# A top-1 expert layer fed by a scan: rows written to their expert places by scatters, read back in order, with routing and weight folding between the last scans

## The chip, the cores and the metric

The kernel runs on one core of a Trainium2 chip. The metric is device time in microseconds (us) of one execution. A core has five engines that run side by side, each working through its own instructions in order and waiting on semaphores for the others: PE (TensorE, matrix multiplies and transposes), DVE (VectorE, elementwise work, reductions and scans), ACT (ScalarE, activation functions and copies), POOL (GpSimd, elementwise work and the issue of indirect DMAs) and SP (SyncE, which here only issues DMAs). SBUF is the on-chip memory of 128 partitions, PSUM the banks into which PE writes, HBM (or DRAM) the memory outside.

## The reference, cut to what matters

The whole program is a chain of eight layers over 2048 tokens of 128 channels: an RG-LRU scan, a local-attention transformer of two blocks, a Mamba layer, a first mixture of experts (top-1 of 32), a chunked attention block, a second mixture of experts, an attention layer with decay and a ternary linear layer. A layer norm stands between layers. The change touches the joint between Mamba and the first experts:

```python
# Mamba, per sequence of 256 tokens: 256 inner channels, 16 states
delta = softplus(delta_raw * w_dt + b_dt)
h = exp(delta * A) * h + delta * B_t * xc        # scan over the tokens
y = sum_n h[n] * C_t[n];  y = y + xc * D_param
out = (y * silu(z)) @ W_out

# first experts: E = 32, capacity C = ceil(1.25 * 2048 / 32) = 80
logits = xt @ w_router
probs  = softmax(logits);  top1 = argmax(probs);  gate = probs[top1]
pos = cumsum(onehot(top1), axis=0)[token, top1] - 1
accepted = pos < C
slot = where(accepted, top1 * C + pos, E * C)
buf = zeros(E * C + 1, H).at[slot].set(xt)       # each token to its place
y = (silu(buf @ w_gate) * (buf @ w_up)) @ w_down # per expert, 80 places
out = xt + where(accepted, y[slot] * gate, 0)
```

The place of a token depends on all tokens before it, so the last tokens' places are known only after the last sequence has passed through Mamba.

## The kernel before

**Layout and stages.** Activations are kept by channel (128 partitions of channels, tokens along the free axis) in fp32. The tokens are 8 sequences of 256, or 16 tiles of 128. Stages follow each other in the program: `rglru`, `local_mamba`, `moe1`, `chunked`, `moe2`, `typed`. In the profiled execution RG-LRU takes 0 to 52 us, local attention with Mamba runs to about 912, the routing of the last tokens, the fetching of rows and the first experts run to about 983, the chunked block to about 1437, the second experts to 1650 and the last two layers to the end. The program text is turned into five instruction streams by a scheduler, which may hoist an instruction within its stream; on the chip every stream runs in order.

**Mamba.** `interleave` mixes the generators of the local blocks (`one_sequence`) with those of `mamba_sequence`, at most two of the latter at a time, by lags written out by hand. In a sequence, `d` (delta) is made by ACT (L747 to L750), finished by four POOL instructions (L752 to L756, the last gives `u`), and then eight steps follow, `m` = 0 to 7. A step needs two broadcast rows `bc` (B and C of two states, read by SP from the small DRAM tensor `xs` of the sequence; three buffers of `bc`), the decay `da` (ACT, L767), three DVE instructions on 128x1024 values (L769 multiply by B, L771 scan, L772 multiply by C) and PE's sum `y`. After the last step come L778 (DVE), L779 (POOL, times the gate `sz`), `wout` (PE), the sum `s` and a layer norm. Its end `x_mamba` is transposed to rows (L790), copied to SBUF and stored to the DRAM tensor `rows1` by `put_rows` (SP), and the router's logits `lg` are computed (L803 copies them out).

**Routing and fetching.** `route1(0, 14)` routes the first 14 tiles, whose logits are in `lg1[0]`, and `route1(14, 16)` the last two. Each finds the largest logit, a one-hot `sel`, the position within its expert by triangular and all-ones matmuls (`cum`), and the place `sc`. To turn places into a list "which token sits in place i" it builds comparison matrices (`ge`, `at`, `column`, `value`) and multiplies them on PE (`which`), giving `index` (L1045). `rows_of` then has POOL fetch the 2560 places as 20 gathers of 128 rows each from `rows1` by `index` (L1112; 12 buffers), and PE transposes each to channels (L1104), with one copy `bt` for four.

**First experts.** `moe1` goes through eight groups of four experts: `pg` and `pu` (gate and up matmuls), `sg` (silu on ACT, multiplied by `pu` on DVE), `py` (down), a copy `ys` and a store to `ybuf`. A group's weights are 768 KB in three DMAs of 256 KB on SP (`weights1`); three buffers hold them, so three groups are loaded ahead and the other five follow as buffers come free. The chunked block begins by gathering each token's result from `ybuf` (POOL, `got<-ybuf,get`), two tiles a sequence, with `combined` adding it to the residual.

**Folding.** The chunked block's attention weights are multiplied together beforehand by `fold` (128 matmul records on PE and eight copies on ACT for two layers, from four raw loads `w_attn` of 1 MB each, plus `less`, 16 records for each layer, and one DVE subtraction `la_res`, `sa_res` for each). In the program text it stands between the two calls of `route1`, behind all sequences; the scheduler moves the parts. `bias_rows` splits a bias into three bf16 parts.

**Loads beside the last sequence.** `among` runs one step of `loads` at each step of the last Mamba sequence: weights of group 0, three raw loads, groups 1 and 2, `w_ffn` (1 MB), and the constants `cst` and `w3`.

Of the kernel before, what the change touches and what calls it, by code (L numbers as in the profile page):

```python
# [20 lines left out]
P = 128  # L21
# [283 lines left out]
class _Kernel:  # L305
    def __init__(self, ctx, tc, ins, out):
# [14 lines left out]

        self.scope = ctx.enter_context(ExitStack())
# [32 lines left out]

        self.get1 = const.tile([P, NT], I32, name="get1")
        self.gate1 = const.tile([P, NT], F32, name="gate1")
        self.sum1 = const.tile([P, 32], BF, name="sum1")
        self.which1 = const.tile([P, 40], F32, name="which1")
        self.index1 = const.tile([P, 20], I32, name="index1")  # L360
# [5 lines left out]
        nc.sync.dma_start(self.w1, ins["w1"])  # L366

# [36 lines left out]

    def exp_ln(self, last=None):

        i = self.nc.scalar.preload_act_table_set("natural_log_exp_and_others")
        if last is not None:
            self.issue_after([i], last)
        self.tc.keep_in_program_order(i)  # L410

# [59 lines left out]
    def rglru(self):  # L471
        nc, tc = self.nc, self.tc
        self.y = self.xs.tile([P, T], F32, tag="x", name="x_rglru")
        with tc.tile_pool(reuse_waits="tile", name="l0", bufs=1) as w, tc.tile_pool(reuse_waits="tile", name="l0t", bufs=2) as wk:

            c1 = self.softplus(w, self.v("apar"), 1, "sp")
            nc.vector.tensor_scalar(self.c12[:, 0:1], c1, -8.0, None, ALU.mult)
            nc.vector.tensor_scalar(self.c12[:, 1:2], c1, -16.0, None, ALU.mult)
            tiles = [w.tile([P, 4, S], F32, name=f"rg{i}") for i in range(4)]
            for _ in self.rglru_group(0, tiles, wk):  # L480
                pass
# [215 lines left out]
    def mamba_sequence(self, b, x, y, na, das, work, scan):  # L697
# [54 lines left out]
        nc.gpsimd.tensor_sub(e, e, t)  # L752
        nc.gpsimd.tensor_add(d, d, e)
        nc.gpsimd.tensor_add(d, d, r)
        u = tile("u", 2)
        nc.gpsimd.tensor_mul(u, d, xc)  # L756
# [22 lines left out]
        nc.gpsimd.tensor_mul(yg, yg, sz)  # L779
# [8 lines left out]
        ps = self.psum("B", "rows")[:, 0:S]  # L788
        for t in range(2):
            nc.tensor.transpose(ps[:, t * P : (t + 1) * P], y[:, b * S + t * P : b * S + (t + 1) * P], self.ident)  # L790
        r = work.tile([P, S], F32, tag="h2", name="rows")
        nc.any.tensor_copy(r, ps)
        self.put_rows(b, r)
        self.logits(b, y, self.w1[:, 834:866], self.lg1[0][:, 2 * b : 2 * b + 2] if b < 7 else self.lg1[1])
        yield 1.0
# [13 lines left out]
    def local_mamba(self):  # L809
        nc, tc = self.nc, self.tc  # L810
        self.rows = self.dram.tile([T, P], F32, name="rows1")
        w = self.w0
        with (
# [4 lines left out]
            ExitStack() as tail,  # L818
# [50 lines left out]
            def then(value):  # L869
                b, z = value  # L870
                if b == 0:

                    self.x = self.xs.tile([P, T], F32, tag="x", name="x_mamba")
                steps = self.mamba_sequence(b, z, self.x, na, das, work, scan)
                return steps if b < 7 else among(steps, loads())

            def loads():

# [3 lines left out]
                raw = self.raw_pool = self.right("raw", tail, 3)  # L882
                self.ws = [self.weights1(0)]
                yield
                self.raw = []
                for i in range(3):
                    self.raw.append(self.raw_weights(raw, i))
                    yield
                for g in range(1, 3):
                    self.ws.append(self.weights1(g))  # L890
                    yield
                self.wf = self.fw.tile([P, 2, 1024], F32, name="w_ffn")
                nc.sync.dma_start(self.wf.rearrange("p l f -> p (l f)"), self.ins["wf"])
                yield
                self.cst = self.fw.tile([P, _C["iota32"][0] - 512], F32, name="cst")
                nc.sync.dma_start(self.cst, self.ins["cst"][:, 512 : _C["iota32"][0]])
                self.w3 = self.fw.tile([P, self.ins["w3"].shape[1]], F32, name="w3")
                nc.sync.dma_start(self.w3, self.ins["w3"])
# [9 lines left out]
            room = self.right("room", tail)  # L908
            self.route1(0, 14, room, small)
            la = self.fold("la", self.fw, lambda: self.raw_weights(self.raw_pool, 3))  # L910
            self.fws = la, self.fold("sa", self.fw)
            self.route1(14, NT, room, small)
# [64 lines left out]
    def route1(self, t0, t1, pools, small):  # L977
# [3 lines left out]
        E, CAP, nb, n = 32, 80, 20, t1 - t0  # L981
        lg = self.lg1[t0 > 0]
        sm = small.tile([P, 8, n], F32, tag="route", name="route", bufs=2)
        mx, ix, pos, ok, sl, sc, part, gate = (sm[:, i, :] for i in range(8))
        each = lambda a, k: a.unsqueeze(2).to_broadcast([P, n, k])
        every = lambda a, k: a.unsqueeze(1).to_broadcast([P, n, k])

        def room(name, dtype, *shape):
            k = int(np.prod(shape))
            t = pools.tile([P, n * k], dtype, tag=f"{name}{n}", name=name)  # L990
            if len(shape) == 1:
                return t.rearrange("p (t e) -> p t e", t=n)
            return t.rearrange("p (t a e) -> p t a e", t=n, a=shape[0])

        oh = room("oh", F32, E)
        nc.vector.tensor_reduce(mx, lg, AX.X, ALU.max)
        nc.vector.tensor_tensor(oh, lg, each(mx, E), ALU.is_equal)
        nc.vector.tensor_tensor(oh, oh, every(self.c("iota32"), E), ALU.mult)
        nc.vector.tensor_reduce(ix, oh, AX.X, ALU.min)
        sel = room("sel", BF, E)  # L1000
# [6 lines left out]
        for t in range(n - 1):  # L1007
            shp = [P, n - 1 - t, E]
            self.mm(cum[:, t + 1 :, :], self.onesb, sel[:, t : t + 1, :].to_broadcast(shp), False, t == n - 2)
        nc.vector.tensor_scalar(sl, ix, float(CAP), float(E * CAP - 1), ALU.mult, ALU.add)  # L1010
        if not t0:
            with nc.allow_low_precision("whole numbers to 14"):
                nc.vector.tensor_reduce(self.sum1, sel.rearrange("p t e -> p e t"), AX.X, ALU.add)
# [6 lines left out]
        ge = room("ge", F32, nb + 1)  # L1020
        nc.vector.tensor_tensor(ge, each(sc, nb + 1), every(self.c("times128"), nb + 1), ALU.is_ge)
        nc.vector.tensor_reduce(part, ge[:, :, 1:nb], AX.X, ALU.add)
        nc.vector.scalar_tensor_tensor(part, part, -float(P), sc, ALU.mult, ALU.add)
        at = room("at", BF, P)
        for t in range(0, n, 4):
            k = min(4, n - t)
            shp = [P, k, P]
            nc.vector.tensor_tensor(
                at[:, t : t + k], self.c("iota128").unsqueeze(1).to_broadcast(shp), part[:, t : t + k].unsqueeze(2).to_broadcast(shp), ALU.is_equal
            )  # L1030
        column = room("column", F32, nb)
        nc.vector.tensor_sub(column, ge[:, :, 0:nb], ge[:, :, 1 : nb + 1])
        value = room("value", BF, 2, nb)
        nc.vector.tensor_scalar(value[:, :, 0, :], column, self.c("number"), None, ALU.mult)
        nc.vector.tensor_mul(value[:, :, 1, :], column, each(self.c("tile")[:, t0:t1], nb))
        which = self.psum("Q", "which")[:, 0 : 2 * nb]
        for t in range(n):
            self.mm(which, at[:, t, :], value[:, t].rearrange("p a b -> p (a b)"), t == 0, t == n - 1)
        if not t0:
            nc.vector.tensor_copy(self.which1, which)  # L1040
        else:
            w = self.which1
# [744 lines left out]
```

## Time and profile before

| | us |
|---|---|
| median of 3 runs (lowest to highest) | 1935.15 (1931.54 to 1938.44) |
| the profiled execution | 1932.07 |
| its span, first to last instruction | 1930.3 |

Over the span PE is busy 1576.3 us (82%), DVE 1076.4 (56%), ACT 1001.7 (52%), POOL 554.6 (29%). The mean granted clock of PE is 0.907 of full speed.

| stretch, us | length | PE busy | DVE busy | ACT busy | POOL busy | PE clock |
|---|---|---|---|---|---|---|
| 0 to 52, RG-LRU | 52.0 | 20.67 | 27.37 | 22.48 | 8.52 | 0.70 |
| 52 to 830, local and Mamba | 778.0 | 602.63 | 535.11 | 538.55 | 281.02 | 0.91 |
| 830 to 864, end of sequence 6, local blocks done | 34.0 | 22.14 | 23.99 | 16.39 | 7.10 | 0.89 |
| 983 to 1437, chunked | 454.0 | 434.86 | 206.37 | 208.45 | 45.81 | 0.98 |
| 1437 to 1650, second experts | 213.0 | 179.47 | 70.84 | 46.91 | 52.96 | 0.90 |
| 1650 to 1930.3, last layers | 280.3 | 245.73 | 154.02 | 137.46 | 133.23 | 0.91 |

The stretches between 864 and 983 are shown with the prediction. A stretch in which one engine is busy nearly all the time is limited by that engine (chunked by PE); a stretch in which none is waits on a chain from engine to engine. The page's view of the chain that ended last covers the end of the program alone and says nothing of the stages touched here.

### The profile page before, as it was taken

The page shows a single profiled execution, that of the slowest core. Times are in us where ns is not written, and L with a number is a line of the kernel's source. Part 1 is how long each engine was busy: PE and PEld are TensorE (multiplying, and loading weights), DVE is VectorE, ACT ScalarE, POOL GpSimd, SP SyncE. Part 2 cuts the span into 40 slices and gives each one's busy share as a digit, 9 for nine tenths or more (in the row PEclk, how much of TensorE's full clock was granted, in tenths as well). Part 3 has the DMA queues.
Part 4 walks back from the last instruction along what each step waited for, and adds up shares of the span by engine and source line. Part 5 has one row for each costly group of instructions (what it writes and reads, how often), then busy time and mean ns, then how long its engine had stood idle before and what let it go on. Part 6 is the DMA issues. An engine that isn't in the chain of part 4 may idle for free. (4 is left out here: it accounts for less than half of the span.)

```text
span 1930.3 us, 28247 instructions
## 1 busy us (share of the span) xinstructions
PE 1576.3 (82%) x10821; PEld 943.1 (49%) x10821; DVE 1076.4 (56%) x1850; ACT 1001.7 (52%) x2650; POOL 554.6 (29%) x491
## 2 busy tenths in 40 slices
PE   3678878888878686657579999999979996898987
PEld 2344544444444443334546666676643652455554
DVE  5734568786969667679123444364353223465654
ACT  4557777767776966543134454444431221454544
POOL 1324452525352223110420111000002133445452
PEclk7689999989999897788689999999989997899998
DMA  3000011111121203172430000000010310000000
GB/s 117 1 1 1 1 40 49 39 53 48 44 58 34 81 16 86 58 221 85 96 106 2 7 7 4 4 2 5 4 39 17 102 43 20 1 4 6 4 6 6
DMA packets 55830, 73.26 MB, mean 38 GB/s; under 512 B 5544, under 2 KB 33840, under 8 KB 54672
## 3 DMA queue, kind: packets, MB, share of 16 engines
q1 hardware_dynamic: 52736, 65.56, 11.6%
q0 software_dynamic: 2960, 5.91, 1.5%
q8 instruction: 85, 1.39, 0.3%
q14 instruction: 49, 0.40, 0.1%
HBM read 65.55 MB, written 6.04 MB: 37 GB/s over the span
## 5 line engine op out<-in xcount | busy, mean ns | idle before, releaser
L393 PE MATMUL y<-hs,ident 128*128 128x512 f32 x256 | 142.5, 685 | 49.5 <-DVE hs L772 49.4
L771 DVE TENSOR_TENSOR_SCAN hs<-da,hs 128x1024 f32<-128x1024 f32 x64 | 150.8, 2364 | 2.2 <-ACT da L767 2.2
L465 PE MATMUL pt<-ident,e 128*128 128x128 f32 x768 | 120.8, 285 | 27.7 <-POOL e L636 17.2
L767 ACT ACTIVATE da<-d,na 128x255 f32<-128x255 f32 x256 | 112.1, 501 | 43.8 <-DVE hs L771 22.1
L1282 POOL TENSOR_TENSOR e<-e,rc 128x512 f32<-128x512 f32 x32 | 33.6, 1050 | 345.9 <-DVE rc L1281 251.4
L1655 ACT ACTIVATE e<-sc,nm 128x128 f32<-128x128 f32 (+1 forms) x256 | 104.1, 435 | 47.6 <-DVE nm L1650 44.9
L1658 POOL TENSOR_TENSOR e<-e,rc 128x1024 f32<-128x1024 f32 x48 | 92.1, 1919 | 112.0 <-DVE rc L1657 68.2
L636 POOL TENSOR_TENSOR e<-e,rc 128x1024 f32<-128x1024 f32 x32 | 70.7, 2210 | 185.9 <-DVE rc L635 185.9
L465 PEld LDWEIGHTS pt<-ident,e 128*128 128x128 f32 x768 | 88.3, 144 | 69.5 <-POOL e L636 23.6
L631 ACT ACTIVATE e<-sc,nm,rn 128x128 f32<-128x128 f32 x256 | 113.5, 465 | 14.7 <-DVE nm L626 14.6
L583 POOL TENSOR_TENSOR t<-t,t 128x512 f32<-128x512 f32 x64 | 90.8, 1419 | 96.1 <-DVE t L570 90.8
L467 ACT COPY ptsb<-pt 128x512 f32<-128x512 f32 x80 | 46.8, 585 | 132.8 <-PE o L393 66.3
L769 DVE TENSOR_TENSOR hs<-u,bc 128x1024 f32<-128x1024 f32 x64 | 83.1, 1304 | 39.7 <-POOL u L756 26.9
L393 PEld LDWEIGHTS y<-hs,ident 128*128 128x128 f32 x256 | 50.4, 212 | 104.8 <-DVE hs L772 61.0
L467 DVE COPY ptsb<-pt 128x512 f32<-128x512 f32 x112 | 75.0, 683 | 40.5 <-PE pt L465 34.5
L1257 ACT COPY kp<-kps 128x512 f32<-128x512 f32 x128 | 74.7, 584 | 39.3 <-PE kps L393 39.0
L393 PE MATMUL qk<-w_local,h 128*128 128x512 f32 x128 | 72.7, 656 | 19.6 <-DVE t L570 13.1
L1650 DVE TENSOR_REDUCE nm<-sc 128x4 f32<-128x1024 f32 (+1 forms) x48 | 58.6, 1221 | 51.4 <-PE sc L393 51.2
L772 DVE TENSOR_TENSOR hs<-hs,bc 128x1024 f32<-128x1024 f32 x64 | 80.4, 1263 | 0.1
L1230 DVE BATCH_NORM_STATS2 st<-out 128x6 f32<-128x128 f32 x80 | 20.0, 287 | 99.3 <-PE out L393 96.2
L1479 ACT ACTIVATE sh<-pg 128x512 f32<-128x512 f32 x32 | 19.1, 597 | 101.3 <-PE pg L393 63.0
L393 PE MATMUL sc<-km,q 64*128 64x512 f32 x192 | 62.9, 724 | 9.3 <-POOL km L1610 8.9
(424 smaller groups left out, 3835.1 us busy)
## 6 DMA issues: line engine op xcount, KB each, us to landing
bc<-xs SPq DMA_DIRECT2D x128, 256.0 KB, 4.7
w_attn<-in_w_dram SPq DMA_DIRECT2D x4, 1024.0 KB, 9.8
w_local<-in_w_dram SPq DMA_DIRECT2D x2, 1557.0 KB, 8.7
w_moe<-in_e1gate_dram SPq DMA_DIRECT2D x8, 256.0 KB, 4.3
w_moe<-in_e1up_dram SPq DMA_DIRECT2D x8, 256.0 KB, 3.6
w_moe<-in_e1down_dram SPq DMA_DIRECT2D x8, 256.0 KB, 4.9
w_moe<-in_e2rg_dram SPq DMA_DIRECT2D x8, 256.0 KB, 3.7
w_moe<-in_e2ru_dram SPq DMA_DIRECT2D x8, 256.0 KB, 3.0
```

The source lines that it names most:

```text
L393: return self.nc.tensor.matmul(out, lhsT, rhs, start=start, stop=stop)
L465: self.last = self.nc.tensor.transpose(pt[:, j * P : (j + 1) * P], src[:, j * P : (j + 1) * P], self.ident)
L467: self.nc.any.tensor_copy(sb.rearrange("p a b -> p (a b)"), pt)
L583: nc.gpsimd.tensor_add(t1, t1, t2)
L631: nc.scalar.activation(e[:, j, g, :], scs[:, j, g, :], AF.Exp, bias=nm[:, j, g : g + 1], scale=rq[:, j, g : g + 1], accum_out=sm[:, j, g : ...
L767: nc.scalar.activation(da[:, n, c, 1:S], d[:, c, 1:S], AF.Exp, scale=na[:, i : i + 1])
L769: nc.vector.tensor_tensor(hs, u.unsqueeze(1).to_broadcast(shp), bn, ALU.mult)
L771: nc.vector.tensor_tensor_scan(line(hs), line(da), line(hs), 0.0, ALU.mult, ALU.add)
L772: nc.vector.tensor_tensor(hs, hs, cn, ALU.mult)
L1257: nc.scalar.copy(k[:, 2 * i : 2 * i + 2, :].rearrange("p a b -> p (a b)"), ps)
L1655: nc.scalar.activation(e[:, i, :], sc[:, i, :], AF.Exp, bias=nm[:, i : i + 1], accum_out=sm[:, i : i + 1])
L1658: nc.gpsimd.tensor_tensor(e, e, rc.unsqueeze(2).to_broadcast([P, n, keys]), ALU.mult)
```

## The change

The diff does these things:

- A DRAM tensor `places1` of 2560 rows is set to zero by one DMA from a zeroed tile at the start (in `rglru`).
- `mamba_sequence` no longer stores rows; the transposes, the copies and `put_rows` of every sequence go. For the last sequence the four finishing instructions of `d` and `u`, and the multiplication by `sz`, are issued on DVE instead of POOL.
- `route1` becomes a generator. It transposes its tiles to rows itself, in fours (`rows`, copied out by ACT), computes the places `put`, and issues one indirect DMA per tile on POOL that writes 128 rows to `places1` at those places (places out of bounds are dropped). `ge`, `part`, `at`, `column`, `value`, `which` and `index` go.
- `beside` runs the loads, both folds and `route1(0, 14)` step by step among the steps of sequences 6 and 7; `route1(14, 16)` follows the last sequence.
- All eight groups of expert weights have buffers of their own: three in `wmoe`, one in `room`, four in `wx`. `cst` and `w3` are loaded in `moe1`'s text.
- `moe1` reads `places1` back in five loads of 512 rows, alternately on SP's and ACT's queue. Each waits for all 16 scatters. The table for silu is loaded after the last exponential of the routing.
- In `chunked`, a sequence that has not been prepared starts with `yield 0.0, 6.0 * b`. The second experts' first weights are requested inside `typed_weights`.

```diff
+            zero = w.tile([P, 512], F32, name="zeros")
+            nc.gpsimd.memset(zero, 0.0)
+            self.cleared = nc.sync.dma_start(
+                self.places1.rearrange("(p g a) d -> p g (a d)", g=5, p=P), zero.unsqueeze(1).to_broadcast([P, 5, 512])
+            )
...
-        nc.gpsimd.tensor_sub(e, e, t)
-        nc.gpsimd.tensor_add(d, d, e)
-        nc.gpsimd.tensor_add(d, d, r)
+        eng = nc.vector if b == B - 1 else nc.gpsimd
+        eng.tensor_sub(e, e, t)
+        eng.tensor_add(d, d, e)
+        eng.tensor_add(d, d, r)
         u = tile("u", 2)
-        nc.gpsimd.tensor_mul(u, d, xc)
+        eng.tensor_mul(u, d, xc)
...
-        nc.gpsimd.tensor_mul(yg, yg, sz)
+        eng.tensor_mul(yg, yg, sz)
...
-        r = work.tile([P, S], F32, tag="h2", name="rows")
-        nc.any.tensor_copy(r, ps)
-        self.put_rows(b, r)
         self.logits(b, y, self.w1[:, 834:866], self.lg1[0][:, 2 * b : 2 * b + 2] if b < 7 else self.lg1[1])
...
+            def beside():
...
+                load, fold, route = loads(), folds(), self.route1(0, NT - 2, self.room, small)
+                for _ in range(3):
+                    next(load, None)
                 yield
+                live = [load, fold]
+                while live:
+                    for g in list(live):
+                        if next(g, True) is True:
+                            live.remove(g)
+                    if route and self.done == B - 2:
+                        live.append(route)
+                        route = None
                     yield
...
+                wx = self.right("wx", self.tail, 4)
+                for g in range(4, 8):
+                    self.ws.append(self.weights1(wx, g))
...
-            room = self.right("room", tail)
-            self.route1(0, 14, room, small)
-            la = self.fold("la", self.fw, lambda: self.raw_weights(self.raw_pool, 3))
-            self.fws = la, self.fold("sa", self.fw)
-            self.route1(14, NT, room, small)
+            for _ in self.route1(NT - 2, NT, self.room, small):
+                pass
...
+        rows = self.y_next.rearrange("p (t d) -> p t d", d=P)
+        for t in range(t0, t1, 4):
+            k = min(4, t1 - t)
+            ps = self.psum("B", "rows")[:, 0 : k * P]
+            for j in range(k):
+                nc.tensor.transpose(ps[:, j * P : (j + 1) * P], self.x[:, (t + j) * P : (t + j + 1) * P], self.ident)
+            nc.scalar.copy(rows[:, t : t + k, :].rearrange("p t d -> p (t d)"), ps)
+        yield
...
+        put = self.put1[:, t0:t1]
+        self.placed = placed = nc.vector.tensor_copy(put, sc)
+        yield
+        for t in range(t0, t1):
+            i = nc.gpsimd.indirect_dma_start(
+                out=self.places1,
+                out_offset=bass.IndirectOffsetOnAxis(ap=self.put1[:, t : t + 1], axis=0),
+                in_=rows[:, t, :],
+                in_offset=None,
+                bounds_check=E * CAP - 1,
+                oob_is_err=False,
+            )
...
+            got = [one.tile([P, 4, P], F32, name=f"got{g}") for g in range(5)]
+            for g, r in enumerate(got):
+                i = (nc.sync, nc.scalar)[g % 2].dma_start(r, self.places1[512 * g : 512 * (g + 1), :].rearrange("(a p) d -> p a d", p=P))
+                for scatter in self.scatters:
+                    self.wait_for(i, scatter)
...
+                if b not in ready:
+                    yield 0.0, 6.0 * b
                     ready[b] = yield from combined(b)
```

## The prediction

> **What bounds the kernel here.** I read the busy tenths over the span first: PE is at nine tenths only in the chunked block, which this change hardly touches. The stages around 912 us show low numbers on all engines. So I cut that stretch up with the busy times by window.
>
> ```profile
> core 0: us, PE busy (x) PEld busy (x) DVE busy (x) ACT busy (x) POOL busy (x), PEclk, DMA share, GB/s
> 864.00:900.60 36.60, 23.18 (x80) 9.93 (x81) 36.60 (x26) 16.23 (x38) 0.00 (x0) 0.78 0.45 134
> 900.60:920.00 19.40, 13.82 (x97) 10.53 (x95) 15.63 (x64) 3.00 (x8) 2.38 (x2) 0.91 0.05 17
> 920.00:983.00 63.00, 33.81 (x212) 30.28 (x212) 6.51 (x14) 12.24 (x21) 23.61 (x26) 0.70 0.60 144
> ```
>
> Three limits follow each other. In the last scan DVE is busy 36.60 of 36.60 us: whatever is put on DVE there lengthens it. Then a chain of short steps. Then 63 us in which no engine is busy for more than 54%. The timelines show the chain:
>
> ```profile
> 857.56 0.22 DVE L803 COPY lg<-lg 128x64 f32<-128x64 f32 x1
> 863.91 1.22 DVE L769 TENSOR_TENSOR hs<-u,bc 128x1024 f32<-128x1024 f32 x1 [1.16 <-POOL u L756]
> 903.37 0.87 DVE L778 SCALAR_TENSOR_TENSOR t<-xc,vec,y 128x256 f32<-128x256 f32 x2 [0.98 <-PE y L393]
> 912.11 0.22 DVE L803 COPY lg<-lg 128x64 f32<-128x64 f32 x1 [0.69 <-PE lg L393]
> ```
>
> ```profile
> 857.80 1.27 POOL L752 TENSOR_TENSOR e<-e,t 128x512 f32<-128x512 f32 x1 [7.99 <-DVE lg L803]
> 859.15 1.52 POOL L753 TENSOR_TENSOR d<-d,e 128x512 f32<-128x512 f32 x1
> ...
> 920.77 1.19 POOL L1112 DMA_INDIRECT got<-rows,index  x1 [1.16 <-DVE bias_part L1215]
> 922.26 0.95 POOL L1112 DMA_INDIRECT got<-rows,index  x1 [0.30 <-issue]
> ```
>
> ```profile
> 924.08 0.45 PE L1104 MATMUL bt<-ident,got 128*128 128x128 f32 x1 [5.98 <-DMA got<-rows,index]
> 930.13 1.83 PE L393 MATMUL pg<-bt,w_moe 128*128 128x80 f32 x8
> 949.51 2.00 PE L393 MATMUL pg<-bt,w_moe 128*128 128x80 f32 x8 [6.70 <-ACT sg L1155]
> 973.61 1.10 PE L393 MATMUL py<-w_moe,sg 128*80 128x128 f32 x8 [0.65 <-DVE sg L1156]
> ```
>
> So: the scan starts at 863.91 and ends at 900.60; the last logits are there at 912.11; POOL starts 20 gathers at 920.77, one per 1.25 us, to 945.7; the experts' matmuls begin at 930.13, wait for rows, and have an idle 6.70 us whose releaser (ACT's `sg`) had itself waited 16.6 us for something the profile calls "remote". The last `ys` is copied at 975.37, and the chunked block's PE work begins at 983.31.
>
> **The sum, step by step.** A pitch is from one start to the next.
>
> *Before the last scan.* The changed order on DVE after the logits' copy (end 857.82) is: largest logit 0.65, one-hot 1.11, its product 1.50, minimum 0.53, `sel` 0.52, between them the four instructions taken from POOL, 128x512 each; DVE's nearest row, `e<-sc,nm` 128x512, has a pitch of 0.61, so 2.44. Together 6.75: the scan would start at 864.57, not 863.91. Ahead of it PE gets eight folds (0.72 per eight records) and three row transposes (0.59 for two): 0 to 3 us, I take 1.0. **+1.7**. ACT's `d` was ready at 857.73 and is needed only 2.4 us later, so two more ACT copies (0.58 each) cost nothing.
>
> *In the last scan.* Eight steps of 4.46 stay. DVE gains: position product and sum 1.27, `sum` 0.81, five small place instructions 0.5, `sa_res` 0.25, two for `get` 0.2, the logits' subtraction 1.60 (before, it ran at 861.08 while DVE waited for POOL: free cover that is gone), gate 1.05. That is 5.7; minimum and `sel`, 1.05, were in there before. **+4.7**. The scan ends near 907.0.
>
> *From scan to logits.* 900.60 to 912.11 was 11.5. `y` needs 2.1 instead of 2.77 (`cum` no longer runs on PE ahead of it), product with `sz` 0.61 on DVE instead of 1.26 on POOL with its handoffs, so `t` to `s` 2.75 instead of 3.50, layer norm 3.6 (3.85, folds and their copies stood in it), logits 1.0 (1.4, ahead of row transposes now). 9.45: **-2.0**.
>
> *From logits to the first `pg`.* It was 18.0. Now: five routing instructions with the copy 1.3; `cum` 0.4 (it waited 1.6 behind `less`, 2.97 us of PE at 912.37, which moves into the scan); seven place instructions 0.9; DVE to POOL 0.85 (919.92 to 920.77); second scatter 1.49 later; its landing: no row has a scatter, the gathers took 3.1 to 3.3 from start to use, so 3.2 (ends 2 and 6); then the loads of 256 KB, 4.3 by the `w_moe` row; four cold transposes and the copy 1.6; handoffs 0.3. Sum 14.3: **-3.7**. The 14 other scatters, 1.25 each, 17.5, start in about the fourth step and lie under the scan on a POOL that is busy 0.00 there; without that cover they would add their 17.5. The new wait, of five loads for all scatters, has `got2`, `got4`, the second experts' weights and the `ybuf` stores queued behind it on SP, and the first `sg` behind it on ACT; all of these need the loaded rows anyway or are needed much later.
>
> *Experts.* 930.13 to 975.37 is 45.2. With rows and weights there, PE's own pitches at full clock (0.85, 0.95, 0.94) are 2.75 a group, the 12 transposes left 1.6 (six took 0.81); the first group is cold, 5.1 (before, the clock rose 5.3 us after steady work began at 949.51); the end 1.7. That is 27.7; with the 0.65 that `py` waited for `sg` in each group 32.9. I take 30.5: **-14.7** (ends -17.5 and -12.3; -8 if the 6.70 stays, which gathers and weight buffers may have caused, though the trace does not say).
>
> *Rest.* Last `ys` to chunked stays at 8. The stagger changes the first 15 us of chunked, where PE's clock is low: **-1.0** (0 to -4). The clearing of 1.31 MB lies in the first 50 us at a DMA share of 0.29: 0. The five groups of weights that were loaded during the experts (3.8 MB) now load beside the last two scans, at a DMA share of 0.45 in 864 to 900: 0, and rival D if not. The removed transposes, copies and stores of sequences 0 to 6 lie where PE is busy 77% and DVE 69%: 0, but the instruction order changes there, so -3 to +3. Moving the folding is worth little: its 128 matmul records already ran at 842.7 to 906.9.
>
> Sum +1.7 + 4.7 - 2.0 - 3.7 - 14.7 - 1.0 = **-15.0**. Against the profiled execution 1932.07 that is 1917.1; it lies 3.1 below the median, so 1920.
>
> **Two rules against rows.** First, the Trainium skill ("SBUF — State Buffer", Who interferes with whom) says that DVE and GpSimd share a port pair as an exclusive lock, the second to issue blocks entirely, and a GpSimd-issued DMA of about 620 ns took about 3100 under a DVE copy. This speaks against scatters under a scan. The rows: POOL's 1.27 became 1.52 beside DVE's routing, and the one gather beside a DVE subtraction took 1.19 instead of 0.94. By the rows 14 x 0.25 = 3.5 on POOL, hidden; by the rule's figure 14 x 3.1 = 43 us, from about 885 to 928, 7 us past the last places. The page also infers that `tensor_tensor` does not starve descriptors. I take the rows. Second, "DMA: Bandwidth & Descriptors" (Anatomy of one DMA) gives about 2.0 us fixed, mostly the write receipt, plus bytes/436e3: scatter and load would be 2.2 + 2.6 = 4.8 in place of my 3.2 + 4.3 = 7.5, 2.7 better; rows here stand above it and decide.
>
> **Rivals.**
> A (0.50): the sum above, own range 1911 to 1928.
> B, larger gain (0.20): no late start (-1.7), experts at PE's own 27.7 (-2.8), DMA as the page prices it (-2.7), chunked -4: about 10 more, 1910. For it: each is an end of a bound. Against: five handoffs had to be ideal.
> C, no change (0.18): each scatter locks DVE out for its own 0.94: 14 x 0.94 = 13.2 us on a DVE without slack, 1933. For it: POOL and DVE slow each other in the rows. Against: 0.25, not 0.94. That folding gains nothing since it was hidden is already in A.
> D, slower (0.12): the broadcast rows come late. Rows of step m+3 are requested when step m's buffer frees, some 6.5 us before use, and land in 4.7; 1.8 to spare. SP now puts the fourth raw load, `w_ffn`, `cst` and `w3`, 2.8 MB, ahead of the first `bc` of sequence 7 (10.8 us at the 263 GB/s of 830 to 842), and weights of groups 4 and 5 ahead of the last; the raw load waits for PE's folds with `xs` and `bc` queued behind. If `bc` lands in 9.8 us like the 1 MB loads, each of eight steps waits 3.3: 26 us, net +11, 1946. It decides from 2 us a step (15/8). For: 0.79 DMA share there already. Against: the expert weights move largely ahead of the scan, and a wait of 4 us once would not decide.
>
> **How the numbers follow.** About 0.3% (5.8 us) is what can be told from no change. Below 1929.3: A nearly whole, B, little of C: 0.70. Within: most of C and edges: 0.18. Above 1941: D: 0.12. The range 1904 to 1938 takes A, B and most of C.
>
> **What would show it.** Right: DVE without gaps from the first `hs` for about 42 us; POOL's scatters below it at about 1 us each; first `pg` about 14 us after the logits' copy; eight groups in about 30 us with no gap; chunked starting near 968. Wrong: `hs` waiting for DMA `bc` (D); DVE instructions of the scan longer than 1.2 and 2.3 (C); the scatter's landing over 6 us; an idle PE within the experts; a different time at 830 us already.

## The result, and the profile after

| us | before | changed | ratio, 95% interval |
|---|---|---|---|
| first comparison | 1935.62 (1931.54 to 1938.44, 4 runs) | 1905.57 (1896.66 to 1908.71, 4 runs) | 0.9839 (0.9801 to 0.9877) |
| second | 1932.45 (17 runs) | 1906.17 (4 runs) | 0.9873 (0.9837 to 0.9909) |
| third, another chip | 1903.86 (9 runs) | 1884.46 (4 runs) | 0.9901 (0.9885 to 0.9916) |

The changed kernel is faster by 30.0, 26.3 and 19.4 us. The forecast was 1920, 15 us less than before, with a range of 1904 to 1938: the direction held, the range held by 1.6 us, and the gain was larger, on the first chip by a factor of two. Which chip the first comparison ran on is not known; it may be that of the second. Chips differ by some 30 us for one kernel, so below totals are compared on one chip or as ratios, and stages by the traces.

First, the busy times by window of the changed kernel, cut at the same events as before: the last scan, the chain behind it up to the last scatter, and from there to the first PE work of the chunked block.

```profile
core 0: us, PE busy (x) PEld busy (x) DVE busy (x) ACT busy (x) POOL busy (x), PEclk, DMA share, GB/s
864.15:904.05 39.90, 27.74 (x92) 13.60 (x91) 39.87 (x41) 16.05 (x38) 15.27 (x9) 0.79 0.56 160
904.05:921.31 17.26, 7.39 (x21) 3.79 (x21) 6.43 (x28) 3.10 (x6) 8.12 (x9) 0.66 0.04 9
921.31:959.43 38.12, 25.89 (x212) 24.93 (x212) 7.29 (x15) 11.41 (x21) 4.51 (x6) 0.81 0.49 134
```

DVE is still busy all through the last scan, now 39.9 us long instead of 36.8, and POOL works under it (15.27 us instead of 0.00). What was a stretch of 63 us with no busy engine has become one of 38 us, in which PE is busy 68%.

The events on DVE's and PE's timelines:

```profile
862.49 0.61 DVE L1027 TENSOR_REDUCE route<-oh 128x14 f32<-128x448 f32 x1
863.02 0.68 DVE L775 TENSOR_TENSOR u<-d,xc 128x512 f32<-128x512 f32 x1
...
914.82 0.23 DVE L817 COPY lg<-lg 128x64 f32<-128x64 f32 x1 [1.15 <-PE lg L396]
...
917.68 0.17 DVE L1055 CAST put<-route 128x2 int32<-128x2 f32 x1
```

```profile
926.15 1.94 PE L1182 MATMUL bt<-ident,got 128*128 128x128 f32 x8 [9.47 <-DMA got<-places]
927.91 1.99 PE L396 MATMUL pg<-bt,w_moe 128*128 128x80 f32 x8
929.69 1.17 PE L396 MATMUL pu<-bt,w_moe 128*128 128x80 f32 x8
930.70 1.06 PE L396 MATMUL pg<-bt,w_moe 128*128 128x80 f32 x8
...
951.82 1.10 PE L396 MATMUL py<-w_moe,sg 128*80 128x128 f32 x8 [0.65 <-DVE sg L1207]
959.43 0.47 PE L1423 MATMUL back<-ident,got 128*128 128x128 f32 x1 [6.51 <-DVE got L1422]
```

The experts start at 927.91 and the last `ys` is copied at 953.59: one row of `pg` at the low clock (1.99 us for what takes 1.06 later), then groups 2.7 us apart, in which PE waits 0.25 us once and 0.65 before the last `py`. Read event by event, and set beside the terms of the prediction:

| stretch | before | after | difference | forecast |
|---|---|---|---|---|
| start to first `hs` of the last scan | 863.91 | 864.15 | +0.2 | +1.7 |
| last scan | 36.8 | 39.9 | +3.1 | +4.7 |
| its end to the logits' copy | 11.4 | 10.8 | -0.7 | -2.0 |
| to the first `pg` | 18.0 | 13.1 | -4.9 | -3.7 |
| experts, first `pg` to last `ys` | 45.2 | 25.7 | -19.6 | -14.7 |
| last `ys` to the chunked block | 7.9 | 5.8 | -2.1 | 0 |
| chunked, first `back` to last logits | 451.4 | 446.2 | -5.2 | -1.0 |
| the rest | 495.6 | 497.4 | +1.8 | 0 |
| span | 1930.3 | 1903.0 | -27.3 | -15.0 |

### The profile page after: what moved, and what is told of

Read it like the earlier page. It is cut to its first block, busy times and chain, and to the rows that moved or that the text cites. A ratio compares the mean times of both kernels' runs of the same rounds, so it can differ in the third digit from the quotient of the medians.

```text
span 1903.0 us, 28168 instructions
## 1 busy us (share of the span) xinstructions
PE 1571.1 (83%) x10805; PEld 944.4 (50%) x10805; DVE 1073.6 (56%) x1830; ACT 1009.9 (53%) x2657; POOL 549.8 (29%) x483
## 5 line engine op out<-in xcount | busy, mean ns | idle before, releaser
L396 PE MATMUL y<-hs,ident 128*128 128x512 f32 x256 | 148.4, 710 | 38.3 <-DVE hs L791 38.3
L786 ACT ACTIVATE da<-d,na 128x255 f32<-128x255 f32 x256 | 112.1, 502 | 36.8 <-DVE hs L790 19.3
L788 DVE TENSOR_TENSOR hs<-u,bc 128x1024 f32<-128x1024 f32 x64 | 86.5, 1360 | 41.3 <-POOL u L775 26.2
L1346 DVE COPY vs<-vps 128x512 f32<-128x512 f32 x64 | 42.3, 671 | 52.5 <-PE out L396 31.1
```

Source lines behind the costliest of these rows:

```text
L396: return self.nc.tensor.matmul(out, lhsT, rhs, start=start, stop=stop)
L786: nc.scalar.activation(da[:, n, c, 1:S], d[:, c, 1:S], AF.Exp, scale=na[:, i : i + 1])
L788: nc.vector.tensor_tensor(hs, u.unsqueeze(1).to_broadcast(shp), bn, ALU.mult)
```

## The experiments

The runs with three weight buffers, without the stagger, with POOL's finish and with late scatters were made on yet another chip, called the fourth here; those of the comparisons are called by their numbers. The kernel before took 1904.72 us there and the changed kernel itself was not run, so those four are set against each other as neighbours. All weights alone, the stagger alone and the late routing ran on the second chip, the three attempts at the end on the third.

**Rows or weights?** The experts' 19.6 us have two candidate causes: rows that are there at once, and weights that are kept. One run gives the changed kernel back its three weight buffers, another gives the kernel before buffers for all weights.

```diff
-                for g in range(1, 4):
-                    self.ws.append(self.weights1(self.wmoe if g < 3 else self.room, g))
+                for g in range(1, 3):
+                    self.ws.append(self.weights1(self.wmoe, g))
...
-                wx = self.right("wx", self.tail, 4)
-                for g in range(4, 8):
-                    self.ws.append(self.weights1(wx, g))
...
-                w = self.ws[g]
+                w = self.ws.pop(0) if self.ws else self.weights1(self.wmoe, g)
```

> The changed kernel with three weight buffers in the first experts, as before, so that groups 3 to 7 are loaded as buffers come free. Theory (the idle 6.7 us and the waits of the experts before came from the gathers; weights alone limit a little): the experts take 29 to 33 us from first pg to last ys (25.7 in the changed kernel, 45.2 before), with no idle of PE over 3 us, so 3 to 7 us slower than the changed kernel. Rival (the weight buffers caused the idle time): 37 us or more, with ACT or PE idle for over 5 us in one piece, 11 us or more slower.

```diff
+            tc.tile_pool(reuse_waits="tile", name="m1x", bufs=5) as self.wx,
         ):
+            ws += [weights(g) for g in range(3, 8)]
...
-        w = self.wmoe.tile([P, 3, 4, P], F32, tag="w", name="w_moe1")
+        w = (self.wmoe if g < 3 else self.wx).tile([P, 3, 4, P], F32, tag="w", name="w_moe1")
```

> The kernel before with five more weight buffers in the first experts, so that no load of weights waits for a buffer; rows are fetched by the 20 gathers as before. Theory (the gathers limit the first half of the experts, the buffers the second): the experts take 36 to 41 us instead of 45.2, since the last four groups run at 2.8 us instead of 3.8, and the idle 6.7 us stays as a wait for rows; 4 to 9 us faster than before. Rival (the buffers alone caused the idle time and the slow groups): 32 us or less, 12 us or more faster.

The stretches in us, each from its own trace:

| | three buffers | all weights |
|---|---|---|
| gathers: experts, and to the chunked block | 45.2 + 7.9 = 53.2 | 39.2 + 5.8 = 45.0 |
| scatters: the same | 29.0 + 9.1 = 38.1 | 25.7 + 5.8 = 31.5 |

Rows by scatter and load save 13 to 15 us, kept weights 7 to 8. Each cell is one trace, and not all are from one chip; PE's low clock alone moves the experts by up to 5 us (see below). A microsecond or two of these differences may be clock. With three buffers and scatters the theory held for the stretch: PE is never idle for more than 0.65 us within the experts, only the later groups are 3.5 to 3.9 us apart again. With gathers and all weights the groups at the end are some 2.9 us apart, and the whole kernel is faster by 5.5 us (1926.96 against 1932.45, ratio 0.9969, 0.9958 to 0.9980), as expected; but the long idle time, which was to stay as a wait for rows, shrinks to 3.41. Part of the gain was given back: the loads of five more groups beside the gathers moved the first `pg` from 18.0 to 20.1 us behind the logits.

The total with three buffers was 1884.31 against 1904.72 before (0.9891, 0.9870 to 0.9912), no worse than the changed kernel's 0.9901 on another chip. Its experts were not slower than those of its neighbours on that chip (28.7 to 31.0 with all weights), because those ran longer at the low clock (see below), and its chunked block was 2 us shorter. So the weights' part in the changed kernel's total is not settled; that in the stretch is. On the second chip 26.3 us of gain stand against 5.5 for the weights alone and 4.7 for the stagger alone (below); the other 16 belong to rows, routing and folding, of which none was run alone.

Most of the 2.1 us behind the last `ys` has to do with the weights too. Two rows of POOL and DVE, kernel before:

```profile
978.79 0.97 POOL L1112 DMA_INDIRECT got<-ybuf,get  x1 [27.82 <-DMA ybuf<-ys]
...
982.96 0.63 DVE L1369 TENSOR_SCALAR got<-got,gate 128x128 f32<-128x128 f32 x2 [9.41 <-DMA got<-ybuf,get]
```

and changed:

```profile
956.48 1.02 POOL L1147 DMA_INDIRECT got<-ybuf,get  x1 [31.77 <-DMA ybuf<-ys]
...
959.09 0.29 DVE L1422 TENSOR_SCALAR got<-got,gate 128x128 f32<-128x128 f32 x1 [7.32 <-DMA got<-ybuf,get]
```

From the gather's start to its use it is 4.2 us before and 2.6 after, which is 1.6 of the 2.1. Before, SP issued five loads of the second experts' weights after the last `ybuf` store (975.78 to 977.80), and the gathers land among them. With kept weights these loads go out earlier (the last at 943.28), and the gather takes 2.6. The two runs agree: 2.6 with all weights, where the loads go early, and 4.6 with three buffers, where the last loads are issued at 961.00, 1.6 us before the gather.

**The stagger of the chunked block** was taken out of the changed kernel, and put alone into the kernel before.

```diff
                 if b not in ready:
-                    yield 0.0, 6.0 * b
                     ready[b] = yield from combined(b)
```

> The changed kernel without the stagger in the chunked block (no yield of 6.0 * b). In the traces the stretch from the first 'back' transposes of the chunked block to the last logits took 451.4 us before and 446.2 after. Theory (the stagger made these 5 us): this stretch is about 451 again and the median about 5 us above the changed kernel's 1905.6. Rival (the 5 us come with the earlier weights, the warmer clock or other reordering): the stretch stays at 446 to 447 and the time is the changed kernel's within 1 us.

> The kernel before with only the stagger of the chunked block added. Theory (the order that the stagger gives to PE's work saves 5 us in the chunked block): 4 to 7 us faster than before, the stretch from the first 'back' to the last logits 445 to 448 us instead of 451.4. Rival (the stagger does nothing without rows and weights being early): within 1.5 us of before.

Without it the chunked stretch is 453.7 us, where three neighbours on that chip take 443.3 to 445.9. With it alone, the kernel before takes 446.2 there, and the kernel before with all weights but no stagger, on the same chip, 453.3. In this stage, which PE bounds, the stagger is thus worth 7 to 10 us between neighbours and 5.2 between the kernel before and the changed one. In the total, with the stagger alone, it is 1927.74 against 1932.45 (0.9980, 0.9963 to 0.9997); without it the changed kernel took 1890.59 against 1904.72 (0.9924, 0.9904 to 0.9944).

Part of this is PE's clock, which the first expectation named as a rival. Added up over windows of 10 us, the granted clock falls short of full speed by 13.5 us without the stagger and by 6.6 to 7.9 in the three neighbours, by 11.6 and 9.8 in the pair of kernels before, and by 9.0 and 8.0 in the first comparison. Taking these off leaves, as an estimate, 2 to 5 us for the order of the work itself. Whether the order brings the better clock with it is open. PE's busy time in the stretch fell from 433.84 to 427.00 us for nearly the same number of matmul records (4687 and 4686). More overlap of small tiles would show like this, and so would the clock; neither was tried by itself.

**DVE or POOL for the last finish of delta.**

```diff
-        eng = nc.vector if b == B - 1 else nc.gpsimd
+        eng = nc.gpsimd
```

> The changed kernel with the four finishing instructions of delta and u, and the product with sz, of the last sequence on POOL again. Theory (DVE's routing instructions were long before, 1.08 to 1.68 us, because POOL worked beside them, and take 0.62 alone): the 128x448 one-hot and product go back to 1.0 us or more, the first hs of the last scan starts only 0 to 2 us later, the product with sz costs 0.7 more; in all 1 to 3 us slower than the changed kernel. Rival (moving these instructions shortened the start by what POOL spends, 5.8 against 2.4): 4 us or more slower, with the routing instructions at 0.62.

DVE's timeline of this run:

```profile
862.69 0.62 DVE L1023 TENSOR_REDUCE route<-lg 128x14 f32<-128x448 f32 x1
863.35 1.26 DVE L1024 TENSOR_TENSOR oh<-lg,route 128x448 f32<-128x448 f32 x1
864.64 1.57 DVE L1025 TENSOR_TENSOR oh<-oh,route_tables 128x448 f32<-128x448 f32 x1
```

and the same two instructions in the changed kernel, where POOL is idle:

```profile
860.22 0.62 DVE L1024 TENSOR_TENSOR oh<-lg,route 128x448 f32<-128x448 f32 x1
...
861.36 0.62 DVE L1025 TENSOR_TENSOR oh<-oh,route_tables 128x448 f32<-128x448 f32 x1
```

The one-hot and its product take two to two and a half times as long when POOL works beside them, and two of POOL's four instructions 1.53 instead of 1.27. The reduction above them keeps its 0.62. The start was 0.95 us later than in the changed kernel (7.43 against 6.48 from the layer norm to the first `hs`), as the theory had it. What it had not was the product with `sz`: on POOL it stands behind the 14 scatters.

```profile
914.16 0.97 POOL L1058 DMA_INDIRECT places<-x_chunked,put  x1 [0.30 <-issue]
915.14 1.29 POOL L798 TENSOR_TENSOR t<-t,sz 128x512 f32<-128x512 f32 x1
```

DVE had `t` ready at 913.62, so the product starts 1.5 us late and takes 0.6 longer. From the scan to the logits it is 15.3 us, 4.5 more than in the neighbours; the other 2.4 are PE's low clock in `y` and `wout` of this run (3.48 and 2.07 us instead of 1.98 and 1.13). By these stretches about 6 us of the gain are gone (0.95, 0.6 in the scan, 4.5), of which 2.4 are the clock; the theory had 1 to 3. The total was 1892.38 against 1904.72 before (0.9932, 0.9912 to 0.9951). If the changed kernel had here the ratio 0.9901 of the third chip, that is 6 us too, but this is an estimate.

**Do the scatters slow the scan?**

```diff
-        for t in range(t0, t1):
-            i = nc.gpsimd.indirect_dma_start(
...
+        if t0:
+            self.scatter(0, t0)
+            self.scatter(t0, t1)
...
+            self.wait_for(i, self.last_step)
```

> The changed kernel with the routing of 14 tiles still inside the last scan, but their scatters held back until the last scan's last DVE instruction. Theory (the scan hides the scatters and they do not slow DVE): the scan from first hs to last takes 39.8 us as now, the 14 scatters take 0.97 + 0.30 each after it, first pg comes 3 to 5 us later, the time is 3 to 5 us longer. Rival (each scatter locks DVE out during its 0.94 us, in part): the scan is 2 us or more shorter, and the time is longer by 0 to 2 us only.

The scan took 39.87 us against 39.90: scatters cost DVE nothing. The first `pg` came 17.1 us after the logits instead of 13.0 to 13.1: the theory held. The total was 1890.53 against 1904.72 before (0.9922, 0.9895 to 0.9948). The other way round POOL does pay. In the changed kernel:

```profile
886.34 2.25 POOL L1058 DMA_INDIRECT places<-x_chunked,put  x1 [35.10 <-DVE put L1055]
888.90 4.01 POOL L1058 DMA_INDIRECT places<-x_chunked,put  x1 [0.30 <-issue]
893.21 1.09 POOL L1058 DMA_INDIRECT places<-x_chunked,put  x1 [0.30 <-issue]
...
896.40 2.36 POOL L1058 DMA_INDIRECT places<-x_chunked,put  x1 [0.30 <-issue]
...
910.31 0.97 POOL L1058 DMA_INDIRECT places<-x_chunked,put  x1 [0.30 <-issue]
918.60 1.43 POOL L1058 DMA_INDIRECT places<-x_chunked,put  x1 [7.31 <-ACT lg L1080]
```

The 14 took from 886.34 to 911.28, 24.9 us instead of the forecast's 17.5, with single ones at up to 4.01 under the scan and 0.97 behind it; the last two places are ready at 917.85, so 6.6 us were to spare. What a scatter waits for can be read by setting DVE's rows beside it:

```profile
889.82 2.29 DVE L790 TENSOR_TENSOR_SCAN hs<-da,hs 128x1024 f32<-128x1024 f32 x1
...
895.71 2.27 DVE L790 TENSOR_TENSOR_SCAN hs<-da,hs 128x1024 f32<-128x1024 f32 x1
```

The scatter that starts at 896.40 ends at 898.76, 0.78 us after the DVE instruction that was running (897.98); the one of 4.01 starts under an earlier instruction, outlasts the next as well and ends 0.80 after it (892.91 and 892.11). All nine that start under the scan end 0.78 to 0.93 us after the end of a DVE instruction with two inputs in SBUF. Two behind the scan that start under a DVE instruction with an input in PSUM (at 906.48 under `t`, at 909.04 under `s`) take 0.97. So in these rows a scatter waits for DVE's running instruction where both its inputs are in SBUF, and DVE does not wait for the scatter. The weight loads that SP issues at the same time are not the cause: with three buffers SP issues none there (DMA share 0.29 instead of 0.56), and the first scatters take 2.25, 4.00, 1.08, 1.52 and 2.35.

**Routing behind the last sequence.** The first batch's routing was moved in the program text behind the last Mamba sequence.

```diff
-                    if route and self.done == B - 2:
-                        live.append(route)
-                        route = None
...
-            for _ in self.route1(NT - 2, NT, self.room, small):
-                pass
+            for t0, t1 in ((0, NT - 2), (NT - 2, NT)):
+                for _ in self.route1(t0, t1, self.room, small):
+                    pass
```

> The changed kernel with the routing of the first 14 tiles and their 14 scatters behind the last Mamba sequence, everything else kept. Theory (the scan of the last sequence is DVE's; routing in it lengthens it by its own 4 us and saves the scatters' 18 us behind it): the scan from the first hs to the last is 35.7 to 36.5 us instead of 39.9, the lead-in from the layer norm of sequence 6 to the first hs about 4 us instead of 6.5, and from the logits to the first pg it takes 18 to 24 us more than 13.1; in all 11 to 17 us slower than the changed kernel. Rival (the routing is nearly free behind the scan, because folds and waits cover it): 6 us or less slower.

This did not make the experiment that was meant: the scheduler hoisted the routing back into the scan, in front of the last step, and the scan took 41.8 us. The 14 scatters ran from 905.33 to 924.51 and were still done before the last places at 927.4, so the first `pg` came 13.2 us after the logits as in the changed kernel. It shows only that the batch may end as late as 3 us before the last places and costs nothing behind them; what the routing in the scan costs was not tried this way. The total was 1913.88 against 1906.17. Of these 7.7 us the scan has 1.9; in the traces most of the difference lies behind the chunked block (498.7 us against 486.9), which the edit does not touch.

**The changed kernel again**, as the second and the third comparison:

> The changed kernel once more, beside the kernel before on the chip of the other experiments. On that chip the kernel before took 1904.7 us, 30.9 less than in the first comparison, and the stages behind the chunked block took about 471 us in four variants instead of 497. If the gain does not depend on the chip, it is 1874 to 1878 here (ratio 0.984); if the stages behind or the experts differ by chip, the experts take 29 us as in the variants and the gain is 4 us or more smaller.

> The changed kernel beside the three versions of this call. On the two chips measured so far it was 26 to 30 us faster than the kernel before; 1880 to 1910 by chip, ratio 0.984 to 0.987.

The first of these did not fall on the fourth chip, as was meant, but on one as slow as the first (1906.17). The other fell on a chip like the fourth (1903.86 and 1904.72 for the kernel before), and the ratio expected for it, 0.984 to 0.987, was missed: it was 0.9901. Why the gain is 19.4 us there and 30.0 on the first is open: there is no trace of the kernel before on that chip.

**Three attempts to do better.** First, the routing's parts that no scatter needs, behind the scan.

```diff
+            after = lambda i, earlier: t0 or self.issue_after([i], earlier)
...
+                    after(nc.vector.tensor_reduce(self.sum1, sel.rearrange("p t e -> p e t"), AX.X, ALU.add), self.last_step)
...
+            after(nc.vector.tensor_reduce(gate, lg, AX.X, ALU.add), self.last_s if not t0 else None)
```

> The changed kernel with those parts of the first batch's routing that no scatter needs (the count by expert, the logits' subtraction, the gates, the clamped places) ordered behind the last scan: the first two behind its last step, the others behind the sum s. Theory (DVE sets the end of the last scan, and is idle in the chain behind it: 2.1 us before y, 3.9 us before the layer norm's end): the scan from first hs to last is 37.2 to 37.6 us instead of 39.9, and the stretch from there to the last logits stays at 10.6 to 11.2, so 2 to 2.7 us faster than the changed kernel. Rival (the moved work is paid back behind the scan, because it stands in front of the last product on DVE or delays it by the exponential on ACT): the stretch to the logits grows by the 2 us that the scan loses.

The moved instructions did fit behind the scan, but the scan took 41.3 us, longer than 39.9. DVE's timeline shows why:

```profile
897.75 1.23 DVE L791 TENSOR_TENSOR hs<-hs,bc 128x1024 f32<-128x1024 f32 x1
902.13 1.22 DVE L788 TENSOR_TENSOR hs<-u,bc 128x1024 f32<-128x1024 f32 x1 [3.16 <-DMA bc<-xs]
```

The new order of the program let SP issue all twelve loads of groups 4 to 7 (3 MB, 887.27 to 896.62) ahead of the last pair of `bc`; in the changed kernel four of them stand ahead of it, and DVE does not wait. This is the mechanism of rival D, for one step and 3.2 us; without that wait the scan would have taken 38.1. The total, 1885.39, is not different from 1884.46. Neither theory described this.

Second, PE kept busy before the experts.

```diff
+        if t0:
+            for _ in range(12):
+                idle = self.mm(self.psum("M", "warm")[:, 0:S], self.ident, self.x[:, (t1 - 2) * P :])
+                self.issue_after([idle], last)
+                last = idle
```

> The changed kernel with twelve matmuls of 128x256 whose results are not read, on PE between the last cum and the first transposes of the fetched rows, where PE is idle for 9.4 to 9.6 us. In six traces of the same code the experts took 25.5 to 31.0 us, with pg at 1.83 to 2.00 us for the first 4 to 14 us and 1.02 to 1.06 after. Theory (that spread is PE's clock, at half after the idle time): the first transposes take 0.82 to 1.0 us for eight in place of 1.94, all pg are at 1.02 to 1.06, the experts take 23 to 24.5 us and the kernel is 1 to 7 us faster, by the chip. Rival (the first groups wait for weights or rows, or the clock falls again in the rest of the idle time): experts as in the changed kernel, time within 1 us.

```profile
918.73 6.98 PE L396 MATMUL warm<-x_mamba,ident 128*128 128x256 f32 x24
928.42 1.68 PE L1187 MATMUL bt<-ident,got 128*128 128x128 f32 x8 [2.71 <-DMA got<-places]
929.92 2.00 PE L396 MATMUL pg<-bt,w_moe 128*128 128x80 f32 x8
...
939.81 1.04 PE L396 MATMUL py<-w_moe,sg 128*80 128x128 f32 x8
```

The second half of the rival came true: the matmuls ended 2.71 us before the rows came. The granted clock was 1.00 at their end, 0.50 from 929.0 on and 1.00 again only from 939. The total was 1884.40 against 1884.46: no gain. The premise stands, though: the spread of the experts' times is PE's clock. The windows of the experts of two runs with the same instructions there, the changed kernel and the one with POOL's finish:

```profile
927.91:953.59 25.68, 24.12 (x205) 23.36 (x204) 5.47 (x11) 10.82 (x20) 0.00 (x0) 0.96 0.51 143
...
937.49:968.47 30.98, 29.42 (x205) 28.66 (x204) 5.47 (x11) 10.82 (x20) 0.00 (x0) 0.79 0.43 119
```

The granted clock is 0.96 and 0.79, and 25.7 us become 31.0.

> The changed kernel with both edits: the parts of the routing that no scatter needs behind the last scan, and the twelve matmuls that keep PE busy. Theory (they act in different stretches): the gains add, 3 to 9 us faster than the changed kernel. Rival (each gain is lost in the next wait, or the later order of PE and DVE changes by the scheduler): no more than the larger of the two.

Both edits together took 1889.64, 5 us more than the changed kernel: the wait for `bc` was 3.97 us. The rival held. None of the three beats the changed kernel on its chip. Three buffers, on another chip, came out level with it (ratios 0.9891 and 0.9901, with overlapping intervals).

## Why the prediction was right, and where it was off

The structure held: the 63 us without a busy engine were a queue of gathers, weights and handoffs; the scan paid for the routing; the scatters went under it. What folding alone is worth no run shows. The number is another matter. By the traces the sum was 12 us short on the first chip, and 1905.57 lies outside rival A's own range of 1911 to 1928; it is nearer to rival B's 1910, which had 0.20. What came is mostly B's list: no late start, experts no slower than PE's own work, DMA below the rows' price and a larger gain in chunked. Six of the eight stretches came out better than their terms, so that the range held, by 1.6 us, is in part luck. By the terms of the sum:

- *Experts, -14.7 for -19.6.* The term "I take 30.5" stood between PE's own 27.7 and 32.9 with the waits for `sg`. It took 25.7. The 32.9 rests on a misreading: not "each group" of the kernel before has the wait of 0.65, but three of eight `py` rows, and a fourth waits 0.96 for a load. After the change the next group's `pg` stands before each `py`, and only two `py` wait, 0.25 and 0.65. The 27.7 was too long as well: the first group, taken as cold throughout at 5.1, took 3.7, because the clock rose within it; in other runs the low clock lasted 3.5 to 15 us. The idle 6.70 us went, and what released it was not found. It was 7.0 in the kernel before with the stagger and 3.4 with all weights, so weights may have a part in it. In both traces with three buffers and gathers ACT's `sg` started 4.29 us after POOL's last gather (944.73 and 949.02 in the kernel before), which points to the gathers as well.
- *Chunked, -1.0 for -5.2.* "The stagger changes the first 15 us" was the wrong picture. The first products came no earlier relative to the block's start (9.6 us before and after); the gain is spread over the later matmuls and their clock, and the runs with and without the stagger show that it comes with the stagger.
- *Last `ys` to chunked, 0 for -2.1.* That the second experts' loads collided with the gathers, and would go out earlier, was in the order of SP's queue and was not costed.
- *Before and in the scan, +6.4 for +3.3.* The routing's pitches 1.11, 1.50 and 1.60 were read from rows beside which POOL was working. Alone they are 0.53 to 0.54. This is 2.6 of the 3.1. The Trainium skill says it ("SBUF — State Buffer", Who interferes with whom): a DVE instruction with two SBUF inputs contends with a POOL instruction that reads SBUF. The rows with POOL's finish agree: 1.26 and 1.57 for 0.62 with two inputs, and no change for the reduction, which has one. The prediction had cited the passage for the scatters and not applied it to its own rows. The 1.0 for PE's folds did not come either: from the layer norm of sequence 6 to the logits' copy it is 1.15 us, before 1.32.
- *Scatters under the scan.* Against that page's 3100 ns I took 1.25 us each by the rows. The nine that started under the scan took 0.97 to 4.01, 1.8 in the mean. That they were hidden was right, with 6.6 us to spare; at 3.1 each they would, by the prediction's own sum, have ended 7 us too late. The inference quoted with it, that `tensor_tensor` does not starve descriptors, did not hold here: a `tensor_tensor` or a scan holds a scatter up until it ends. Rival C, a scan slowed by the scatters, is refuted by 39.87 against 39.90.
- *From logits to the first `pg`, -3.7 for -4.9.* The term "landing 3.2 and load 4.3" was 1.7 too long: from the start of the last scatter (920.34) to the first transposes 5.8 us passed instead of 7.5, nearer to 4.8, the prediction's estimate from the DMA page's rule. The page gives that rule for DMAs that GpSimd issues, and the loads go out on SP and ACT.
- *Tail, -2.0 for -0.7.* `y` and the way from `t` to `s` came as forecast (2.1 and 2.8 us). The layer norm, from `s` to its end, took 4.7 instead of the forecast's 3.6: its two PE rows took 1.22 us each, where they took 0.70 before, at a granted clock of 0.55 instead of 1.00 (from `s` to the layer norm's end). This was not in the sum. Why the clock is lower there was not tried.
- *Earlier sequences, 0.* On the first chip the layer norm of sequence 6 comes at 857.7 us instead of 856.2; this 1.4 takes back a lead to the scan that is 1.2 us shorter (6.5 for 7.7). On the second chip it comes at 862.3 and 864.0 in two traces of the changed order and at 852.5 and 854.9 in two of the old. The difference begins early: from the layer norm of sequence 0 to that of sequence 1 it is 95.2 us or more in the changed order and 90.5 to 90.8 in the old. The -3 to +3 named such a shift and the zero did not hold it. What causes it was not tried.

Rival D decided nothing in this kernel, but its mechanism is one reordering away.

## What to carry to other kernels

The length of an instruction in a trace, taken while another engine worked beside it, is not its price: look at what ran beside it before taking it into a sum. Where one stage fetches through a queue, ask what its last loads collide with in the next stage. When work is moved into a stretch that one engine bounds, the order of the load queue is part of the move: one pair of broadcast rows behind 3 MB of weights took back what 2 us of DVE had gained.

## What the runs showed of the hardware that was not expected

- After 9.5 us of idle time PE's matmuls ran at half speed (`pg` 1.91 to 2.00 us instead of 1.02 to 1.06) for 3.5 to 15 us, by run, with the same instructions. 7 us of matmuls, then 2.7 us of idle time, were not enough to keep the clock up: it was granted at 1.00 when work resumed and at 0.50 within 0.6 us.
- An indirect write issued by POOL took 0.97 us beside an idle DVE. Under DVE's scan it ended 0.78 to 0.93 us after the end of a DVE instruction, and so took up to 4.01 us, while DVE's instructions kept their length. POOL's `tensor_tensor` beside DVE's slowed both (1.53 us for 1.27, and 1.26 to 1.57 for 0.62).
- One kernel differs by some 30 us from chip to chip. In the traces of the first and second chip the stages behind the chunked block take 487 to 499 us, in those of the third and fourth 471 to 475. Some 20 us of it are one pause in the second experts, with PE idle 9.5 us in one piece for nothing that the profile shows, on the first and second chip and not on the others.
